# Row maxima of causal attention: the diagonal blocks masked on GpSimd after a copy by ScalarE, instead of by a matmul on TensorE

## The chip, the cores and the metric

The kernel runs as one program on one core of a Trainium2 chip. The metric is the device time of one execution in microseconds (us); the time of a kernel is the median of its runs. A profile is one further execution, recorded instruction by instruction. The engines are named as the profile names them: PE (TensorE, with PEld for its weight loads), DVE (VectorE), ACT (ScalarE), POOL (GpSimd) and SP (SyncE, which issues DMAs here).

## The reference

Two layers over 4096 tokens of width 256 (16 sequences of 256). Each layer adds to its input the output of a mixer and of a mixture of experts, both fed with the same layer norm. Layer 0 has a cumulative mixer with a gated unit and 32 experts of which a token takes four; layer 1 has causal attention with 16 heads of width 16 and eight experts of which a token takes two, and a shared one. The change lies in layer 1's attention, cut here to what matters:

```python
Q = (Xn @ Wq_w.T + Wq_b).reshape(b, s, H, D_K).transpose(0, 2, 1, 3)   # H = 16, D_K = 16, s = 256
K = V = Q
Qr = Q * cos + _rotate_half(Q) * sin
Kr = K * cos + _rotate_half(K) * sin
A = jnp.einsum('bhqd,bhkd->bhqk', Qr, Kr) / math.sqrt(D_K)
A = jnp.where(causal, A, -jnp.inf)
A = jax.nn.softmax(A, axis=-1)
O = jnp.einsum('bhqk,bhkd->bhqd', A, V)
```

The softmax needs, for each head and each query, the maximum of the scores over the keys that are not later than the query. Of a head's 256 x 256 scores in blocks of 128, the block of early queries and late keys is never needed, the block of late queries and early keys is needed whole, and the two blocks on the diagonal (a head's "own halves") are needed below the diagonal.

## The kernel before, in words

Tokens are worked in eight groups `g` of 512, each of two sequences `b`. All work is written as generators that yield steps: an engine, a cost in us, and options. `Weave` is a planner that runs when the kernel is built. It keeps a clock for each engine and takes, again and again, the step that can begin first, the smaller key at ties (`rush` lowers a step's key for such ties). Within a generator a step begins when the one before it has landed, which is its cost and a hop of 0.15 us later, unless that one is `aside`. `need` and `gives` are events, `get` and `put` are pools of buffers. The planned order is the order in which instructions stand on each engine, and engines work in order; semaphores hold an instruction until its inputs are there. Where a ready step asks for two or more of a pool, steps with a larger key may not take from that pool from the time it is ready (`first` and `behind`).

The pools that matter: `s`, the eight PSUM banks, and `mid`, 14 buffers of SBUF with 2 KB for each of 128 partitions. The experts' tiles take both: in layer 1 each of three lanes runs `expert_tile1` (transposes at L1207, `xhi` and `xlo` at L1212 and L1215, matmuls at L1229, `st` at L1240 to L1244, `thi` and `tlo` at L1247 and L1250, matmuls at L1256, `ry` at L1266, scatters of `y` on POOL at L1277), with `xr` gathered by POOL at L1185, three tiles ahead. Layer 0's dense part (`gated`, matmuls at L942 and L919, `sg` at L964 to L968) and the gathers of `yk` (L1054), the scatters of `perm` (L571, each behind a memset of one column at L570) and `combine` run beside the first groups' attention.

Attention of one `g, b` is `project`, then for each of four columns `c` (four heads) `maxima`, then `shifts`, which adds the maxima to the queries, and for each `c` `weigh`, which forms the scores anew with keys on the partitions (L1457), their exponentials (ACT, L1468), sets those above the diagonal to zero by a selection on POOL (L1474), multiplies by the values (L1486) and copies the result out (ACT, L1502; in the last group's second sequence DVE, L1497 and L1499). `shares` then divides by the sums by way of DMAs.

`maxima` takes four banks. Eight matmuls (L1408), one for each head and half of the queries, write a head's scores into the 384 columns of its bank: columns 0 to 127 are the early queries' own half, 128 to 255 the late queries against the early keys, 256 to 383 the late queries' own half. `masked` then adds for each head, by one bf16 matmul of `ident_b` with `mask_b` (L1397), 0 or -1e30 to the two own halves. DVE reduces each bank's three blocks to three maxima (L1419), which go to `tops`, and the bank is free. In `shifts` the late queries' two maxima are put together (L1437).

The generators' keys set the mix: `maxima` of `g, b, c` has 39 + 10 g + 4.5 b + 0.8 c, the experts' lanes of layer 1 begin at 70 and rise.

Of the kernel before, what the change touches and what calls it, by code (L numbers as in the profile page):

```python
# [13 lines left out]
ALU = mybir.AluOpType  # L14
AX = mybir.AxisListType
PSUM = bass.MemoryType.PSUM

P = 128
# [27 lines left out]
NEG = -1e30  # L46
# [161 lines left out]
def step(eng, cost, **o):  # L208
    return eng, cost, o
# [3 lines left out]
def two_layers(  # L213
# [6 lines left out]
    nc = tc.nc  # L220
# [27 lines left out]
    def mid(shape, name, dtype=F32):  # L248
        return work.tile(shape, dtype, tag="mid", name=name, bufs=MID)
# [3 lines left out]
    def bank(shape, i=0):  # L253

        n = shape[1] if len(shape) == 2 else shape[1] * shape[2]
        ap = banks[w.ids["s"][i]][: shape[0], :n]
        return ap if len(shape) == 2 else ap.rearrange("p (a b) -> p a b", a=shape[1])
# [16 lines left out]
    ident_b = const.tile([P, P], BF16, name="ident_b")  # L274
    mask_b = const.tile([P, 2 * P], BF16, name="mask_b")
# [17 lines left out]
    tops = [const.tile([P, H, 3], F32, name=f"tops{i}") for i in range(2)]  # L293
# [71 lines left out]
    RUSH = 40.0  # L365
# [929 lines left out]
    def rows_of(r):  # L1295
        return slice(HW * r, HW * (r + 1))
# [93 lines left out]
                nc.tensor.transpose(tp[:, i, j * P : (j + 1) * P], flat[:, j, c : c + P], ident)  # L1390
        return tp

    def masked(four, lhsT, rhs):

        for s in four:
            ends = s.rearrange("p (i n) -> p i n", n=P)[:, 0::2, :]
            nc.tensor.matmul(ends, lhsT=lhsT, rhs=rhs, start=False, stop=True)  # L1397

    def maxima(g, b, c):

        need = [("kT", g, b, c // 2), ("qT", g, b, c // 2)]
        yield step("PE", 1.4, get=["s"] * 4, need=need)
        kT, qT = qks[g, b]
        four = [bank([P, 3 * P], r) for r in range(4)]
        for i in range(2):
            n = (i + 1) * P
            for r in range(4):
                nc.tensor.matmul(  # L1408
                    four[r][:, i * P : i * P + n],
                    lhsT=qT[rows_of(r), c, i * P : (i + 1) * P],  # L1410
                    rhs=kT[rows_of(r), c, :n],
                    start=(i == 0),
                    stop=False,
                )
        masked(four, ident_b, mask_b)
        for r in range(4):
            yield step("DVE", 0.48, put=["s"], gives=[("max", g, b, c)] if r == 3 else [])

            nc.vector.tensor_reduce(  # L1419
                tops[b][:, c * 4 + r, :],  # L1420
                four[r].rearrange("p (i n) -> p i n", n=P),
                AX.X,
                ALU.max,
            )

    def shifts(g, b):


        for two in range(HC // 2):
            yield step("DVE", 0.43, need=[("max", g, b, 2 * two + i) for i in range(2)])  # L1430
            hs = slice(8 * two, 8 * two + 8)
            to = lambda j: peaks[:, j, :].rearrange("p (r w) -> p w r", w=HW)[
                :, 2 * two : 2 * two + 2, :
            ]
            of = lambda i: tops[b][:, hs, i].rearrange("p (c r) -> p c r", r=4)
            nc.vector.tensor_copy(to(0), of(0))
            nc.vector.tensor_tensor(to(1), of(1), of(2), ALU.max)  # L1437
            yield step("PE", 0.35, get=["s"])
            tp = bank([P, S])
            for j in range(2):  # L1440
                nc.tensor.transpose(tp[:, j * P : (j + 1) * P], peaks[:, j, :], ident)
            yield step("DVE", 0.61, put=["s"], gives=[("mT", g, b, two)])
            qT = qks[g, b][1][:, 2 * two : 2 * two + 2, :]
            nc.vector.tensor_tensor(  # L1444
                qT, qT, tp.unsqueeze(1).to_broadcast([P, 2, S]), ALU.add
            )
# [284 lines left out]
    for g in range(NG):  # L1731
# [3 lines left out]
        for b in range(GT // S):  # L1735
            at = DENSE[g] + 5 * b
# [32 lines left out]
    for g in range(NG):  # L1769
        early = max(DENSE[g] + 9, 34) + 0.5 * g  # L1770
        w.add(chosen(g), early)
        w.add(combine(g), early, 0.1)
        w.add(route1(g), early + 2, 0.1)
        w.add(spread(L1, g), early + 4)
        at = 38 + 10 * g
        w.add(room(g), at - 6)
        for b in range(GT // S):
            ab = at + 4.5 * b
            w.add(project(g, b), ab)
            for c in range(HC):  # L1780
                w.add(maxima(g, b, c), ab + 1 + c * 0.8)
                w.add(weigh(g, b, c), ab + 5 + c * 0.8)
            w.add(shifts(g, b), ab + 4.5)
            w.add(shares(g, b), ab + 8)
        w.add(half(g), at + 9)
        ready = [("aT", g, 0), ("po", g, 1, HC - 2)] if g == LAST[0] else [("aT", g, 1)]
        w.add(opened(NG + g, "o1", 2, ready), at + 12)
        for c in range(NC1):
            w.add(chunk(g, c), at + 12 + c)
        w.add(unpacked(g), at + 10)  # L1790
        w.add(attended(g), at + 14)
        w.add(closed1(g), at + 15)
        if g < LATE:
            w.add(finish(g), 130)
# [81 lines left out]
```

## Time and profile before

| | |
|---|---|
| median of 6 runs | 1654.29 us (1648.11 to 1661.16) |
| the profiled execution | 1666.46 us |
| its span, first to last instruction | 1664.0 us |
| mean granted TensorE clock | 0.910 |
| instructions in the span | 27711 |
| matmuls on PE | 9372 |
| mask matmuls (L1397) | 256 |
| reductions of maxima (L1419) | 256, from 788.6 to 1606.4 us |
| selections in `weigh` (L1474) | 64, from 823.4 to 1628.8 us; 1087 ns at least, median 1094, 1972 at most |
| layer 1's experts (L1207) | from about 1248 us on |

The page gives for each engine its busy time and share of the span. A group of instructions shows the line, engine and operation, the tile written and the tiles read, the shape and the number, then busy us and mean ns of one, and behind the second bar how long the engine had been idle just before them and what ended that. A window's row shows the busy time of each engine in that stretch and the granted clock, as a share of the full one. Matmuls overlap in PE's pipeline, so that the mean duration of one is longer than the distance from one to the next.

### The profile page before, as it was taken

Reading aid. Unit: us, or ns where it says so; the run is one execution under the profiler, and the core shown is the slowest. Engines: PE = TensorE matmul, PEld = TensorE weight load, DVE = VectorE, ACT = ScalarE, POOL = GpSimd, SP = SyncE. Lnnn points to the kernel's source line nnn. Section 1 sums busy time; section 2 is a strip of 40 time slices with the busy share of each in tenths; the row PEclk is TensorE's granted clock in tenths of the full one; section 3 lists DMA queues with packets and bytes.
Section 4 is the critical chain, followed back from the end, with each engine's and each line's share of the span. In section 5 each row is a group of like instructions: output and inputs, shape, how many; then the busy total and the mean of one; then the engine's idle time right before and its main releaser. Section 6 shows DMA issues by size and latency. Waiting matters only on the chain. (4 is left out here: it accounts for less than half of the span.)

```text
span 1664.0 us, 27711 instructions
## 1 busy us (share of the span) xinstructions
PE 1407.9 (85%) x9372; PEld 1117.9 (67%) x9372; DVE 972.6 (58%) x2505; ACT 693.3 (42%) x1521; POOL 829.3 (50%) x1086
## 2 busy tenths in 40 slices
PE   5889969889999997787799699786878888899975
PEld 3678857568898886666567587553546777777753
DVE  4988937574342432148847373675755575565757
ACT  4333312444564553223324132442344756664641
POOL 3477854564554552436663614354145556555530
PEclk8999989989999998888889799886879999898997
DMA  9211100258888888415532502243244344343368
GB/s 328 77 52 39 39 26 14 59 185 260 277 278 265 265 248 192 153 59 161 93 80 90 143 26 90 65 111 59 89 96 137 105 140 138 122 129 117 97 203 266
DMA packets 164069, 223.45 MB, mean 134 GB/s; under 512 B 29672, under 2 KB 120152, under 8 KB 163672
## 3 DMA queue, kind: packets, MB, share of 16 engines
q1 hardware_dynamic: 136152, 162.11, 31.8%
q0 software_dynamic: 27776, 59.58, 13.6%
q8 instruction: 74, 1.21, 0.3%
q14 instruction: 67, 0.55, 0.1%
HBM read 151.13 MB, written 66.22 MB: 131 GB/s over the span
## 5 line engine op out<-in xcount | busy, mean ns | idle before, releaser
L942 PE MATMUL bank<-yT,wsw 128*128 128x256 f32 x1024 | 244.3, 385 | 4.6 <-issue 3.5
L571 POOL DMA_INDIRECT perm<-pairs,at_u x192 | 192.3, 1002 | 95.5 <-DVE pairs L514 40.6
L744 POOL DMA_INDIRECT xr_ring<-rows_d,who x160 | 155.7, 973 | 158.3 <-PE bank L762 113.5
L942 PEld LDWEIGHTS bank<-yT,wsw 128*128 128x128 f32 x1024 | 194.6, 194 | 34.2 <-issue 7.1
L1474 POOL TENSOR_SCALAR_AFFINE_SELECT pT<-pT 128x1024 f32<-128x1024 f32 x64 | 72.9, 1141 | 218.9 <-ACT pT L1468 182.0
L919 PE MATMUL bank<-wdn,sg 128*128 128x256 f32 x512 | 136.9, 416 | 50.0 <-DVE sg L968 46.5
L1419 DVE TENSOR_REDUCE tops<-bank 128x3 f32<-128x384 f32 x256 | 131.2, 548 | 58.5 <-PE bank L1397 36.6
L1054 POOL DMA_INDIRECT yk<-y,slots x128 | 132.6, 1036 | 61.8 <-issue 35.6
L919 PEld LDWEIGHTS bank<-wdn,sg 128*128 128x128 f32 x512 | 103.4, 208 | 73.6 <-DVE sg L968 53.4
L1468 ACT ACTIVATE pT<-bank 128x384 f32<-128x384 f32 x256 | 110.8, 499 | 95.2 <-PE bank L1457 61.5
L767 DVE COPY xTr<-bank 128x512 f32<-128x512 f32 x80 | 54.4, 689 | 138.9 <-PE bank L762 97.9
L1277 POOL DMA_INDIRECT y<-ry,to x78 | 80.9, 1038 | 93.6 <-ACT ry L1266 81.0
L1408 PE MATMUL bank<-kT,qT 32*128 32x128 f32 (+1 forms) x1024 | 97.2, 400 | 32.9 <-ACT aT L1502 12.3
L964 ACT ACTIVATE sg<-bank 128x512 f32<-128x512 f32 x64 | 38.0, 596 | 146.2 <-PE bank L942 84.2
L1408 PEld LDWEIGHTS bank<-kT,qT 32*128 32x128 f32 x1024 | 58.4, 210 | 58.3 <-issue 19.4
L351 PE MATMUL bank<-wqkvsu,xnT 128*128 128x512 f32 (+1 forms) x256 | 97.4, 514 | 0.0
L1457 PE MATMUL bank<-qT,kT 32*128 32x256 f32 (+1 forms) x1024 | 76.6, 380 | 23.9 <-DVE qT L1444 12.0
L1185 POOL DMA_INDIRECT xr<-rows_d,who x78 | 79.0, 1013 | 31.5 <-issue 20.4
L1229 PE MATMUL bank<-xhi,w_ring 128*88 128x256 f32 x312 | 87.0, 308 | 5.7 <-issue 3.1
L798 ACT ACTIVATE ry<-bank,share 128x256 f32<-128x256 f32 x160 | 66.8, 470 | 50.7 <-PE bank L788 19.7
L1457 PEld LDWEIGHTS bank<-qT,kT 32*128 32x128 f32 x1024 | 56.8, 203 | 45.5 <-DVE qT L1444 12.6
L1229 PE MATMUL bank<-xlo,w_ring 128*88 128x256 f32 x312 | 83.0, 297 | 2.7 <-DVE xlo L1215 1.9
(270 smaller groups left out, 3241.6 us busy)
## 6 DMA issues: line engine op xcount, KB each, us to landing
w_ring<-in_wud SPq DMA_DIRECT2D x80, 256.0 KB
vones<-in_wud SPq DMA_DIRECT2D x80, 256.0 KB
y<-ry SPq DMA_DIRECT2D x80, 256.0 KB
w_b<-in_we SPq DMA_DIRECT2D x39, 304.0 KB
rows_d<-xn SPq DMA_DIRECT2D x16, 512.0 KB
xnT<-xnT_d SPq DMA_DIRECT2D x16, 512.0 KB
y1k<-y SPq DMA_DIRECT2D x16, 512.0 KB
x<-in_x SPq DMA_DIRECT2D x8, 512.0 KB
```

Source lines behind the costliest of these rows:

```text
L351: nc.tensor.matmul(ps_ap, lhsT=lhs(k), rhs=rhs(k), start=(k == 0), stop=(k == KC - 1))
L571: ins = nc.gpsimd.indirect_dma_start(out=la.perm, out_offset=bass.IndirectOffsetOnAxis(ap=la.at_u[:, c : c + 1], axis=0), in_=la.pairs[:, ...
L744: nc.gpsimd.indirect_dma_start(out=xr_ring[:, m % 3, i * D : (i + 1) * D], out_offset=None, in_=rows_d, in_offset=bass.IndirectOffsetOnAxi ...
L919: nc.tensor.matmul(oTs[o][j][:, t % 2, :], lhsT=lhs[:, t * P : (t + 1) * P] if lhs.shape[1] > P else lhs, rhs=rhs, start=(done == 0 and t ...
L942: nc.tensor.matmul(ap[:, i, :], lhsT=w_of[0](i, k), rhs=rhs[:, k, :], start=(i == 0 and k == 0), stop=(i == 1 and k == KC - 1),)
L1054: nc.gpsimd.indirect_dma_start(out=ys[g, k][:, t, :], out_offset=None, in_=y0, in_offset=bass.IndirectOffsetOnAxis(ap=L0.slots[:, c : c + ...
L1229: nc.tensor.matmul(h[:, c, :], lhsT=w_c(i // 2), rhs=(hi, lo)[i % 2][:, i // 2, :], start=(i == 0), stop=(i == n - 1),)
L1277: ins = nc.gpsimd.indirect_dma_start(out=y1, out_offset=bass.IndirectOffsetOnAxis(ap=L1.to[:, i, m : m + 1], axis=0), in_=y[:, i, :], in_o ...
L1408: nc.tensor.matmul(four[r][:, i * P : i * P + n], lhsT=qT[rows_of(r), c, i * P : (i + 1) * P], rhs=kT[rows_of(r), c, :n], start=(i == 0), ...
L1419: nc.vector.tensor_reduce(tops[b][:, c * 4 + r, :], four[r].rearrange("p (i n) -> p i n", n=P), AX.X, ALU.max,)
L1457: nc.tensor.matmul(four[r][:, q : q + n], lhsT=kT[rows_of(r), c, i * P : (i + 1) * P], rhs=mT[rows_of(r), c, i * P :], start=(i == 0), sto ...
L1468: nc.scalar.activation(pT[:, :, r, :], four[r].rearrange("p (b n) -> p b n", n=P), AF.Exp)
```

## The change

The mask matmuls go. The score matmuls of a call end with the late queries' ones. Then, for each of the four heads, ACT copies the two own halves out of the bank into a `mid` buffer that two heads share (`own`), and DVE reduces the middle block alone, straight from the bank, into the second of the head's three maxima; then the bank is free. For each pair of heads POOL selects in place, in the 512 elements of `own`, what is not above the diagonal and fills the rest with -1e30, and one reduction on DVE takes the first and third maximum of both heads at once. A call asks for two `mid` buffers with its four banks, and its planned costs are 0.95 us on PE (1.4 before), four times 0.37 on ACT, four times 0.22 and twice 0.65 on DVE (four times 0.48 before) and twice 0.62 on POOL, with `rush`.

```diff
-    def masked(four, lhsT, rhs):
-
-        for s in four:
-            ends = s.rearrange("p (i n) -> p i n", n=P)[:, 0::2, :]
-            nc.tensor.matmul(ends, lhsT=lhsT, rhs=rhs, start=False, stop=True)
-
     def maxima(g, b, c):
 
         need = [("kT", g, b, c // 2), ("qT", g, b, c // 2)]
-        yield step("PE", 1.4, get=["s"] * 4, need=need)
+        yield step("PE", 0.95, get=["mid", "mid"] + ["s"] * 4, need=need)
...
-                    stop=False,
+                    stop=(i == 1),
                 )
-        masked(four, ident_b, mask_b)
+
+        owns = [mid([P, 2, 2, P], "own") for _ in range(2)]
         for r in range(4):
-            yield step("DVE", 0.48, put=["s"], gives=[("max", g, b, c)] if r == 3 else [])
-
-            nc.vector.tensor_reduce(
-                tops[b][:, c * 4 + r, :],
-                four[r].rearrange("p (i n) -> p i n", n=P),
-                AX.X,
-                ALU.max,
-            )
+            of = four[r].rearrange("p (i n) -> p i n", n=P)
+            own = owns[r // 2]
+            yield step("ACT", 0.37, gives=[("own", g, b, c, r // 2)] if r % 2 else [])
+            nc.scalar.copy(own[:, r % 2, :, :], of[:, 0::2, :])
+
+            yield step("DVE", 0.22, put=["s"])
+            nc.vector.tensor_reduce(tops[b][:, c * 4 + r, 1:2], of[:, 1:2, :], AX.X, ALU.max)
+        for two, own in enumerate(owns):
+            yield step("POOL", 0.62, need=[("own", g, b, c, two)], rush=RUSH)
+            flat = own.rearrange("p r i k -> p (r i) k")
+            nc.gpsimd.affine_select(
+                out=flat, in_=flat, pattern=[[0, 4], [-1, P]],
+                compare_op=ALU.is_ge, fill=NEG, base=0, channel_multiplier=1,
+            )
+            yield step("DVE", 0.65, put=["mid"], gives=[("max", g, b, c)] if two else [])
+            at = c * 4 + 2 * two
+            nc.vector.tensor_reduce(tops[b][:, at : at + 2, 0:3:2], own, AX.X, ALU.max)
```

`ident_b` and `mask_b` are still loaded at the start.

## The prediction

> **What bounds the kernel now.** I read the page's first part, then the stages by window, the groups by line and form, the waits of PE, and the timeline of two calls of `maxima`. The page says which engine is nearest to full:
>
> ```profile
> PE 1407.9 (85%) x9372; PEld 1117.9 (67%) x9372; DVE 972.6 (58%) x2505; ACT 693.3 (42%) x1521; POOL 829.3 (50%) x1086
> ```
>
> A share over the whole span mixes stages, and the first maxima come at 787 us, the last at 1606. The windows table cuts the rest there (start and end, length, busy us of PE, PEld, DVE, ACT, POOL with instruction counts, granted clock, DMA share, GB/s):
>
> ```profile
> 787.00:900.00 113.00, 99.24 (x701) 73.42 (x700) 74.43 (x224) 40.35 (x83) 70.90 (x89) 0.88 0.46 98
> 900.00:1050.00 150.00, 125.52 (x762) 98.03 (x760) 69.72 (x201) 37.69 (x70) 58.69 (x72) 0.92 0.28 80
> 1050.00:1250.00 200.00, 156.07 (x1378) 106.40 (x1378) 140.11 (x403) 83.37 (x174) 78.11 (x95) 0.81 0.33 84
> 1250.00:1610.00 360.00, 320.46 (x2889) 258.52 (x2889) 223.72 (x405) 215.99 (x425) 193.93 (x257) 0.92 0.40 125
> 1610.00:1664.00 54.00, 25.17 (x216) 17.85 (x216) 33.53 (x35) 7.08 (x15) 4.85 (x4) 0.75 0.88 284
> ```
>
> PE is busy 0.88, 0.84, 0.78 and 0.89 of the first four stages, 64 calls lie in them (8, 8, 20 and 28), and no other engine passes 0.70. So PE is the bound, loosely where the granted clock is 0.81 and tightly from 1250 us. The groups by line and form price the instructions that matter (busy us, mean ns of one | idle before, releaser):
>
> ```profile
> L1419 DVE TENSOR_REDUCE tops<-bank 128x3 f32<-128x384 f32 x256 | 131.2, 548 | 58.5 <-PE bank L1397 36.6 <-remote 11.7 <-issue 9.5
> L1474 POOL TENSOR_SCALAR_AFFINE_SELECT pT<-pT 128x1024 f32<-128x1024 f32 x64 | 72.9, 1141 | 218.9 <-ACT pT L1468 182.0 <-issue 29.9 <-PE bank L1397 6.4
> L1397 PE MATMUL bank<-mask_b,ident_b 128*128 128x256 bf16 x256 | 45.8, 310 | 0.0
> L1486 PEld LDWEIGHTS bank<-pT,vones 128*32 128x32 f32 x1024 | 29.0, 116 | 46.3 <-issue 17.6 <-POOL pT L1474 10.7 <-POOL apart L570 7.5
> L1502 ACT COPY aT<-bank 128x256 f32<-128x256 f32 x60 | 22.4, 373 | 96.2 <-PE bank L1486 54.9 <-remote 19.8 <-PE bank L1229 9.5
> L550 DVE TENSOR_REDUCE pl<-oa 128x16 f32<-128x512 f32 x8 | 5.4, 680 | 0.1
> ```
>
> The timeline shows what a call's four mask matmuls hold (start us, us, engine, idle before in brackets):
>
> ```profile
> 1356.85 0.94 PE L1408 MATMUL bank<-kT,qT 32*128 32x128 f32 x16
> 1357.72 0.33 PEld L1397 LDWEIGHTS <-ident_b 128*128 128x128 bf16 x4 [0.33 <-issue]
> 1357.72 0.61 PE L1397 MATMUL bank<-mask_b,ident_b 128*128 128x256 bf16 x4
> 1358.09 0.36 PE L1229 MATMUL bank<-xhi,w_ring 128*88 128x256 f32 x1
> ```
>
> The next work starts at 1358.09, 0.37 us after the first mask matmul, although the four are drawn 0.61 long. The 0.33 ahead of them is the change from 32-row pieces to the full array; whatever full-array work comes next pays it too, so it stays.
>
> **PE's saving.** 256 mask matmuls go. By busy time they are 45.8 us. From the first mask matmul of each call to the start of the next matmul, read in the timeline for all 64 calls, the slots are 5.6, 4.7, 13.0 and 14.4 us in the four stages, 37.6 together; from first to fourth alone, 26.0. A slot saved is worth time only where PE would have been busy: by the shares above 5.6 x 0.88 + 4.7 x 0.84 + 13.0 x 0.78 + 14.4 x 0.89 = 31.8 us. That is the credit; 26.0 by the same shares gives 22.
>
> **What is added.** ACT: four copies a call of a head's two own halves, 128x256 out of a bank, at L1502's 373 ns: 256 x 0.373 = 95.5 us. POOL: two selections a call over 512 elements; L1474's median is 1094 ns for 1024, so between half of that with no fixed part (0.55) and 0.60 with the 0.11 us that a one-element memset on POOL takes (L570); I take 0.60: 128 x 0.60 = 77 us. DVE: instead of four reductions at 548 ns (2.19 us), four over 128 elements and two over 512. L1161's reductions of 64 elements take a median of 0.21, which is the floor; the straight line from there to L1419's 384 gives 0.28 for 128. L550 has 0.68 for 512. At 0.28 a call is 2.48 us, 0.29 more, 19 us in all; at 0.21 it is the same as before. I take 19.
>
> None of this work is on PE, and each engine has room (between 787 and 1610 us DVE is 62% busy, ACT 46%, POOL 49%). It is not free, because PE waits for these engines. From the waits of PE between 787 and 1610 us, it waits 53 us for DVE, 32 for ACT and 9.5 for POOL (the rows summed by engine), while they work 508, 377 and 402: 0.10, 0.084 and 0.024 us for each busy us. At those rates the added work costs 19 x 0.10 + 95.5 x 0.084 + 77 x 0.024 = 11.8 us, say 12. If the cover is poorer, with twice the rates, it is 24; if the earlier release of the banks outweighs it, nothing.
>
> **The new wait.** A masked maximum on DVE needs POOL's selection, and that needs two ACT copies. Behind a held maximum on DVE stand `xlo`, `st`, `tlo` and `sg` of the experts and the dense part, whose banks and operands PE waits for. POOL's selections wait in order as well; behind one stand the gathers of `xr` and `yk` and the scatters of `y`. With `xr` fetched three tiles ahead I cost that at nothing; without that cover it is up to 0.60 us for each. For DVE's hold the trace has no row. From below it is nothing (the selection was done long ago), from above 1.0 us or more, a selection behind one of POOL's DMA instructions of about 1.0 us. The nearest row is L1486, where weights wait for the same kind of selection: 10.7 us over 64, 0.17 each. That makes 128 x 0.17 = 21 us of hold on DVE. Between the 0.10 above (2 us) and all of it (21), I let 9 us reach PE, since DVE sits in every chain that frees banks.
>
> **Order and buffers.** `maxima` yields ACT, DVE, ACT, DVE and so on, each after the one before it has landed, so the planner's own call is longer: by its costs and its hop of 0.15, four reductions took 2.5 us behind PE and now the copies and reductions take 3.6, the selections with their maxima 3.1 more. Maxima run well ahead of `weigh`, which hides that, except for the last four calls at 1597 to 1606 us, where about 1.5 us come on top of the tail. Two `mid` buffers are held in a call; counted from first write to last read in the timeline, six to eight of the 14 are in use from 1250 us on, so I cost them at nothing. But the planner reserves what is asked for twice, and a `maxima` that waits for banks now also keeps `mid` from steps of later keys. With every cost changed, the whole order behind 787 us is dealt anew. What such a deal is worth the waits of PE show: single waits of 11.1 us (L1408 for `aT`), 9.4 (L1457 for `over`, behind an addition that waits for its DMA) and 9.3 (L919 for `sg`). I take nothing for it and allow 12 us to both sides.
>
> **The clock.** The stage with most calls for its work, 1050 to 1250 us, already has 0.81. If it fell to the 0.75 of the last row, its 156 us of PE would become 12 longer; if it rose to 0.88, 12 shorter. I take no change. [...]
>
> **Ports.** L1474's selections take 1087 ns at least and 1141 on average, so company on DVE costs 0.05 each, 6 us over 128 on POOL, which are covered. [...]
>
> **The sum.** 31.8 - 12 - 9 - 1.5 = 9.3 us off. The profiled execution is 1666.46 us (span 1664.0, 2.5 around it), 12.2 above the median of the six runs, 1654.29; the difference is taken over as it is, since the stages are the same: 1657.2 for that execution, 1645 for the median.
>
> **The rivals.** No change: the slots were only 26.0 and fall partly into waits, credit 22, against the same 22.5: 1655. For it speaks the loose stage at 0.81; against it 0.89 from 1250 us.
>
> Slower: DVE held by the masked maxima. POOL is busy 0.49 of the time between 787 and 1610, mostly in instructions of 1.0 us, so a selection comes 0.25 us late on average on top of the 0.17: 0.42 x 128 = 54 us of hold, of which three quarters reach PE, 40. Without the hold the change gains 18.3, so 1654.3 - 18.3 + 40 = 1676. It decides from 0.21 us for each of the 128 masked maxima that reach PE (18.3 + 8.3 = 26.6 us): then the time is up by over 0.5%. For it speak POOL's 182 us of waiting for ACT at L1474; against it the earlier release of banks.
>
> More than forecast: the added work is all covered and the hold is nil, 31.8 - 4: 1626. ACT's 0.44 speaks for it, the waits for `aT` against it.
>
> **Chances.** Forecast 0.34, more than forecast 0.10, no change 0.24, slower 0.32. About 0.5% (8.3 us) is what a measurement of this kernel can tell from no change. The range goes from the larger gain to the slower case with the 12 us of the order, less what is left out at both ends: 1624 to 1684; the likeliest case alone is 1633 to 1646.
>
> **What would show it.** Right: no L1397; PE some 46 us less busy with 9116 matmuls; 256 copies on ACT near 0.37, 128 selections on POOL near 0.60, DVE up by 10 to 20 us; PE's share between 1250 and the last maxima still above 0.85. The slower case: long idle times of DVE ahead of the masked maxima with POOL as releaser, and PE waiting for `sg`, `xlo`, `tlo` or banks. Wrong altogether: a stage whose clock has moved by over 0.05, or a tail behind the last maxima that is 10 us longer.

## The result, and the profile after

The kernel after takes 1677.53 us (median of 20 runs, 1662.18 to 1693.36), the kernel before beside it 1653.49 (46 runs, 1638.78 to 1665.1): a ratio of 1.0153 [1.0133, 1.0173] (in brackets, here and below, the 95% interval). The change makes the kernel about 24 to 25 us slower, where 9.3 us off were forecast. The time lies inside the range, and near the 1676 of the slower rival, but the experiments below show that it did not come about in that rival's way.

The profiled execution of after took 1674.32 us (span 1672.6), 3 below its median; that of before took 1666.46, above its median. So these two traces show only 8 of the 24 us. Their shapes can be compared; the sizes are taken from the timed runs.

The first part of the page after:

```profile
PE 1426.5 (85%) x9116; PEld 1129.3 (68%) x9116; DVE 995.6 (60%) x2633; ACT 768.5 (46%) x1777; POOL 916.1 (55%) x1214
```

256 matmuls are gone, and yet PE is busy 18.6 us longer, not 46 less. ACT has 75 us more, POOL 87, DVE 23. The windows table of after, with the cuts used for before (start and end, length, busy us and count of PE, PEld, DVE, ACT, POOL, granted clock, DMA share, GB/s); the last row ends 10 us later than before's:

```profile
787.00:900.00 113.00, 96.84 (x617) 70.62 (x609) 67.88 (x189) 45.58 (x106) 75.64 (x94) 0.73 0.36 79
900.00:1050.00 150.00, 131.28 (x791) 105.51 (x784) 87.40 (x267) 53.02 (x112) 66.96 (x86) 0.92 0.35 100
1050.00:1250.00 200.00, 158.02 (x1288) 110.78 (x1286) 135.61 (x399) 102.08 (x243) 105.99 (x137) 0.77 0.32 87
1250.00:1610.00 360.00, 312.58 (x2606) 247.60 (x2606) 217.72 (x433) 237.00 (x509) 218.02 (x301) 0.89 0.40 124
1610.00:1674.00 64.00, 42.66 (x348) 28.62 (x347) 46.32 (x64) 16.57 (x41) 17.04 (x12) 0.63 0.69 221
```

The clock column is the thing to see. Where before had 0.88, 0.92, 0.81, 0.92 and 0.75, after has 0.73, 0.92, 0.77, 0.89 and 0.63. The same matmul took longer at the lower clock (the 64 of 32x256 of `weigh` in the first stage, L1457 before and L1461 after: 461 ns on average at 0.88, 587 at 0.73), and that is where PE's busy time comes from. From the first maxima to the end, in one row for each kernel, before ahead of after:

```profile
787.00:1700.00 913.00, 726.46 (x5944) 554.23 (x5942) 541.50 (x1266) 384.48 (x766) 406.49 (x516) 0.88 0.38 110
```

```profile
777.00:1700.00 923.00, 748.03 (x5686) 567.79 (x5685) 564.20 (x1393) 458.42 (x1020) 492.59 (x642) 0.83 0.37 108
```

These windows end behind the kernel, and the time behind its end counts in them as full clock. Up to the end of its span PE idles for 150.5 us before and 147.6 after. Its busy time, each stretch weighted with the clock granted in it, is 649 us of work at the full clock before and 624 after. So PE has less work, idles as long, and is busy for 21.6 us more, because more of its work fell into times of a lower clock.

The groups that took the place of the mask matmuls (busy us, mean ns of one | idle before, releaser):

```profile
L1422 POOL TENSOR_SCALAR_AFFINE_SELECT own<-own 128x512 f32<-128x512 f32 x128 | 90.3, 712 | 41.7 <-ACT own L1415 40.4
L1415 ACT COPY own<-bank 128x256 f32<-128x256 f32 x256 | 88.5, 379 | 43.1 <-PE bank L1402 26.9
L1418 DVE TENSOR_REDUCE tops<-bank 128x1 f32<-128x128 f32 x256 | 70.8, 282 | 57.6 <-ACT own L1415 44.1
L1428 DVE TENSOR_REDUCE tops<-own 128x4 f32<-128x512 f32 x128 | 85.9, 677 | 12.7 <-POOL own L1422 8.9
```

The durations are those foreseen, but for the selections (712 ns on average, where 600 were taken). The last line is the rival's own place, and it is nearly empty: DVE idled 12.7 us ahead of the masked maxima, 8.9 of it for POOL. DVE idled longer ahead of the small reductions, 44.1 us for ACT's copies. Before, the group in that place (L1419) waited 36.6 us for PE.

The first transposes of layer 1's experts (L1207) run from 1240 to 1574 us (before from 1248 to 1585) and end 11 us earlier; what lies behind them takes 99 us instead of 79. The last four token groups start their scores 114 us apart on average (before, 105), and the last maximum starts at 1636.5 us instead of 1606.4, with the last scores of `weigh` at 1644 instead of 1627. Up to the experts' start nothing was lost: 787 to 1248 before, 777 to 1240 after.

PE's waits in the same stretch as in the prediction, 787 to 1610 us, add up to 76.5 us for DVE (before 53), 22.7 for ACT (32) and 5.7 for POOL (9.5). The longest entries (us in total, times, longest us):

```profile
PE bank L919 <- DVE sg L968: 15.3, 3, 7.6
PE bank L1461 <- DVE qT L1448: 9.3, 5, 4.0
PE bank L1402 <- ACT qT L1381: 7.4, 1, 7.4
PE bank L1445 <- DVE peaks L1441: 6.7, 4, 5.0
```

PE waits in them for `sg`, `qT` and the peaks, a few long waits each. None of its waits in this stretch names the masked maxima (L1428); those for the middle blocks' maxima (L1418) sum to 6.1 us, against 5.9 for the maxima before (L1419).

### The profile page after: what moved, and what is told of

Read it like the earlier page. It is cut to its first block, busy times and chain, and to the rows that moved or that the text cites. A ratio compares the mean times of both kernels' runs of the same rounds, so it can differ in the third digit from the quotient of the medians.

```text
span 1672.6 us, 27994 instructions
## 1 busy us (share of the span) xinstructions
PE 1426.5 (85%) x9116; PEld 1129.3 (68%) x9116; DVE 995.6 (60%) x2633; ACT 768.5 (46%) x1777; POOL 916.1 (55%) x1214
## 5 line engine op out<-in xcount | busy, mean ns | idle before, releaser
L1402 PE MATMUL bank<-kT,qT 32*128 32x256 f32 (+1 forms) x1024 | 102.3, 419 | 27.6 <-ACT qT L1381 7.4
L1461 PE MATMUL bank<-qT,kT 32*128 32x256 f32 (+1 forms) x1024 | 102.3, 431 | 23.9 <-DVE qT L1448 11.8
L1422 POOL TENSOR_SCALAR_AFFINE_SELECT own<-own 128x512 f32<-128x512 f32 x128 | 90.3, 712 | 41.7 <-ACT own L1415 40.4
L1461 PEld LDWEIGHTS bank<-qT,kT 32*128 32x128 f32 x1024 | 74.0, 236 | 57.2 <-issue 18.0
L1415 ACT COPY own<-bank 128x256 f32<-128x256 f32 x256 | 88.5, 379 | 43.1 <-PE bank L1402 26.9
L1418 DVE TENSOR_REDUCE tops<-bank 128x1 f32<-128x128 f32 x256 | 70.8, 282 | 57.6 <-ACT own L1415 44.1
L1402 PEld LDWEIGHTS bank<-kT,qT 32*128 32x128 f32 x1024 | 63.1, 223 | 51.3 <-issue 17.4
L1428 DVE TENSOR_REDUCE tops<-own 128x4 f32<-128x512 f32 x128 | 85.9, 677 | 12.7 <-POOL own L1422 8.9
```

Of the source, the lines that this page charges most:

```text
L1402: nc.tensor.matmul(four[r][:, i * P : i * P + n], lhsT=qT[rows_of(r), c, i * P : (i + 1) * P], rhs=kT[rows_of(r), c, :n], start=(i == 0), ...
L1415: nc.scalar.copy(own[:, r % 2, :, :], of[:, 0::2, :])
L1422: nc.gpsimd.affine_select(out=flat, in_=flat, pattern=[[0, 4], [-1, P]], compare_op=ALU.is_ge, fill=NEG, base=0, channel_multiplier=1,)
L1428: nc.vector.tensor_reduce(tops[b][:, at : at + 2, 0:3:2], own, AX.X, ALU.max)
L1461: nc.tensor.matmul(four[r][:, q : q + n], lhsT=kT[rows_of(r), c, i * P : (i + 1) * P], rhs=mT[rows_of(r), c, i * P :], start=(i == 0), sto ...
```

## Experiments

The theories were: (M) the credit for the masks is small or absent, since PE is paced by its clock and by others' chains; (A) the work added on ACT, POOL or DVE costs more than its share; (O) the re-dealt order costs; (H) DVE is held by masked maxima behind POOL, the rival. Every ratio is to runs of the kernel before on the same chip. The runs are spread over five chips: on two of them the kernel before takes 1490 us (mean clock 0.948), on three 1652 to 1674 (0.911 to 0.916), so ratios are compared, not times, and a comparison of two chips is weaker than one on the same chip. Where a run is said to have the order of before or of the changed kernel, its trace has it: DVE, ACT and POOL take the instructions that both kernels have in the same order, and PE does but for a few score matmuls that change places with a neighbour.

### The masks alone

**nomask_old_order** and **nomask_again** (the same kernel on two chips): the kernel before without its mask matmuls, in before's order.

```diff
-                    stop=False,
+                    stop=(i == 1),
-        masked(four, ident_b, mask_b)
```

> The kernel before without its 256 mask matmuls and with nothing in their place, so that the maxima are taken over the unmasked diagonal blocks; the planned costs and the order are those of before. It tells what PE's saving alone is worth. By the prediction's credit it is 22 to 32 us faster than before, 1622 to 1632. [...] If the credit stands, the whole loss must come from what was added or from the order.

> The kernel before without its mask matmuls once more, with more rounds, on the same chip as the three others: it is the base for the run with the copies from a constant. 0.9935 as before, between 0.989 and 0.998. Its granted clock lies about 0.010 below that of before, as in the first run; the prediction's credit, 0.981 to 0.987, is excluded if the interval stays above 0.988.

Measured: 0.9935 [0.9891, 0.998] on the first chip, 11 us; 0.9996 [0.9973, 1.0019] on the second, nothing. The mean granted clock fell with it both times: 0.8994 against 0.9106, and 0.9365 against 0.948. The row from the first maxima to the end on the first chip:

```profile
793.00:1700.00 907.00, 704.66 (x5686) 542.71 (x5685) 539.07 (x1265) 383.93 (x764) 405.89 (x514) 0.87 0.39 110
```

The masks took 21.8 us of busy time with them (726.5 to 704.7). Weighted with the clock as above it is 649 to 621, so 28 us of work at the full clock, near the 26.0 that lay between first and fourth mask matmul. About 11 of these became time on the first chip and none on the second; both intervals exclude the 22 of the low credit. So M holds: most of the credit was never there.

**nomask_new_cost**: the same, with the plan told the shorter PE step.

```diff
-        yield step("PE", 1.4, get=["s"] * 4, need=need)
+        yield step("PE", 1.00, get=["s"] * 4, need=need)
```

> The same without masks, but the planner is told 1.0 us for the score matmuls of a call where it was told 1.4, so that the order behind the first maxima is dealt anew; no operation is added. It tells what a new deal is worth with the same work. By the prediction's allowance it lies within 12 us of the one with the old order. If a new deal alone can cost the 24 us that were lost, it can lie as far above.

Measured: 1.002 [0.9978, 1.0063]. One planned cost, and with it another deal of the order, takes back the 0.65% that leaving out the masks gave (the medians of the two runs, on the same chip, lie 13 us apart).

**after_filled** is the other direction: the changed kernel, with eight matmuls of 128 columns a call into an unused part of the banks, as many columns as the four masks had.

```diff
+        for i in range(8):
+            spare = banks[w.ids["s"][i % 4]][:, 3 * P :]
+            nc.tensor.matmul(spare, lhsT=ident_b, rhs=mask_b[:, :P], start=False, stop=(i >= 4))
```

> The changed kernel, and behind the scores of each call eight bf16 matmuls of 128x128 by 128 columns into the unused last quarter of the four banks, where the mask matmuls stood: as many columns for PE as the masks, with no use. Same plan. If PE's work were what counts (the prediction's credit), it is 22 to 32 us slower than the changed kernel. [...]

**after_again** and **after_third** are the changed kernel as it is, the first in this set.

> The changed kernel as it is, so that its ratio to before is known on the chip that the next three runs have. Both theories expect 1.013 to 1.022.

> The changed kernel as it is, on the chip of the run beside it. 1.015 to 1.022 of before.

Measured: after_filled 1.0154 [1.0082, 1.0225], after_again 1.0174 [1.0096, 1.0251], after_third 1.0165 [1.0118, 1.0213]. Useless columns put back on PE cost nothing that four runs of each can tell: the medians of after_again and after_filled, on the same chip, are 1678.2 and 1678.6 us, which excludes the 22 to 32 us of the credit but not a cost of some 10. The mean clock rose by 0.014 (0.9053 against 0.891). after_filled, then after_again, from the first maxima on:

```profile
770.00:1700.00 930.00, 773.55 (x6225) 596.41 (x6225) 569.46 (x1411) 462.70 (x1026) 499.72 (x651) 0.86 0.39 110
```

```profile
770.00:1700.00 930.00, 740.45 (x5712) 564.45 (x5711) 568.61 (x1407) 461.47 (x1026) 497.23 (x650) 0.85 0.39 109
```

PE is busy for 33 us more. These two profiled executions are 16.8 us apart (1685.86 and 1669.05), though the medians agree, so the traces put 16 of the 33 us into gaps that PE had anyway; by the timed runs it is all of them, within some 10 us.

### The order alone

**old_ops_new_order**: the steps, costs and buffers of the changed kernel, with the mask matmuls and one reduction over three blocks as before. ACT's, POOL's and the last DVE steps are planned and hold nothing.

```diff
             yield step("ACT", 0.37, gives=[("own", g, b, c, r // 2)] if r % 2 else [])
-            nc.scalar.copy(own[:, r % 2, :, :], of[:, 0::2, :])
             yield step("DVE", 0.22, put=["s"])
-            nc.vector.tensor_reduce(tops[b][:, c * 4 + r, 1:2], of[:, 1:2, :], AX.X, ALU.max)
+            nc.vector.tensor_reduce(tops[b][:, c * 4 + r, :], of, AX.X, ALU.max)
...
             yield step("POOL", 0.62, need=[("own", g, b, c, two)], rush=RUSH)
-            nc.gpsimd.affine_select(
...
```

> The changed kernel's steps, costs, buffers and so its planned order, but the operations of before: the mask matmuls behind the scores, one reduction of three blocks where the middle block's stands; the copies, selections and pair maxima are steps with nothing in them. Theory one (the order): the loss is in the order, with attention's last groups behind the experts; then it is as slow as the changed kernel or slower by the mask matmuls, 1675 to 1700. Theory two (the operations): the loss is DVE, ACT and POOL holding each other; then it is near before, 1645 to 1665.

Measured: 1.0173 [1.0086, 1.0259], with not one new instruction. Its row from the first maxima on has as many instructions as before's, and PE busy for 760.2 us instead of 726.5, for nearly the same work at the full clock (656 us, before 649) and as much idle time (151.7 and 150.5):

```profile
786.00:1700.00 914.00, 760.19 (x5942) 575.32 (x5941) 538.75 (x1265) 385.73 (x764) 404.18 (x514) 0.86 0.38 109
```

Its planned costs (0.95 and 0.22) are not those of its operations, though, which could be the reason by itself. Two more runs set that apart.

**old_ops_newer_order**: the same without the two `mid` buffers that a call reserves.

```diff
-        yield step("PE", 0.95, get=["mid", "mid"] + ["s"] * 4, need=need)
+        yield step("PE", 0.95, get=["s"] * 4, need=need)
```

> The changed kernel's steps and planned costs with the operations of before, as in the run old_ops_new_order (1.0173), but the two mid buffers of a call are not asked for, so that nothing is kept from steps with later keys beyond the banks. If the reservation made the order bad, it is at 1.005 or below; if the planned row of ACT, DVE, POOL and DVE steps did, it stays at 1.012 or more.

**old_ops_row**: the kernel before with its own operations and costs, and only the longer row in the plan: an empty ACT step ahead of each reduction, two empty POOL steps and the later `max` behind them.

```diff
-            yield step("DVE", 0.48, put=["s"], gives=[("max", g, b, c)] if r == 3 else [])
+            yield step("ACT", 0.37)
+            yield step("DVE", 0.48, put=["s"])
...
+        for two in range(2):
+            yield step("POOL", 0.62, rush=RUSH)
+            yield step("DVE", 0.0, lat=0.8, gives=[("max", g, b, c)] if two else [])
```

> The operations of before with their right planned costs (1.4 us on PE, 0.48 for each reduction), and with the change's extra steps planned between and behind them, empty: 0.37 on ACT ahead of each reduction, twice 0.62 on POOL, and the maxima there 0.8 us behind each of these. The runs old_ops_new_order and old_ops_newer_order had costs in the plan that their operations did not have (0.95 on PE, 0.22 on DVE). If the longer row of steps makes a bad order, this one is at 1.008 or more of before; if those were slow since their plan was wrong on PE and DVE, it is at 1.003 or below.

Measured: old_ops_newer_order 1.013 [1.0095, 1.0164], old_ops_row 1.013 [1.0092, 1.0167]. Without the reservation of `mid` the planner deals the same order on DVE, ACT and POOL, so the reservation did not make it, and old_ops_new_order and old_ops_newer_order show one order to be slow on two chips. The order of old_ops_row is another one: with the right costs a longer row can be dealt as badly, 1.3% or 21 us. That does not show that the row made the changed kernel's order slow, since in nomask_new_cost one planned figure cost 0.8%.

**before_late_max**: the kernel before, whose plan has a call's maxima come 3.7 us later, and nothing else.

```diff
-            yield step("DVE", 0.48, put=["s"], gives=[("max", g, b, c)] if r == 3 else [])
+            yield step("DVE", 0.48, put=["s"])
...
+        yield step("idle", 0.0, lat=3.7, gives=[("max", g, b, c)])
```

> The kernel before with nothing changed but one figure in the plan: the event that the maxima of a call are there comes 3.7 us later, which is what the change's longer row of steps adds by the planner's costs. Same operations, same costs of each. Theory one, sharpened: the next group's attention of a sequence may only start when this group's has ended (the at0 and at1 buffers), so that a later maximum lengthens the period of the groups; then this is slower than before by over 0.5%, with 110 us or more from one group's scores to the next behind 1250 us, where before has 103 to 108. If latency is covered, as the prediction had it, it is within 0.5%.

Measured: 0.9938 [0.9908, 0.9968], faster. The later maxima are not what costs. What is left of the row is ACT's and POOL's time in the plan and the longer hold of the four banks there, or the chance of one deal; which of them it is was not told apart.

### The operations alone, in before's order

**new_ops_old_order**: before's plan, with all the new operations: the four copies stand right behind the scores, the reductions in before's four DVE steps, and selection and shared maximum behind each second one.

```diff
-                    stop=False,
+                    stop=(i == 1),
-        masked(four, ident_b, mask_b)
...
+        owns = [mid([P, 2, 2, P], "own") for _ in range(2)]
+        for r in range(4):
+            ends = four[r].rearrange("p (i n) -> p i n", n=P)[:, 0::2, :]
+            nc.scalar.copy(owns[r // 2][:, r % 2, :, :], ends)
         for r in range(4):
             yield step("DVE", 0.48, put=["s"], gives=[("max", g, b, c)] if r == 3 else [])
-            nc.vector.tensor_reduce(tops[b][:, c * 4 + r, :], ...)
+            nc.vector.tensor_reduce(tops[b][:, c * 4 + r, 1:2], of[:, 1:2, :], AX.X, ALU.max)
+            if r % 2:
...
+                nc.gpsimd.affine_select(out=flat, in_=flat, ...)
+                nc.vector.tensor_reduce(tops[b][:, at : at + 2, 0:3:2], own, AX.X, ALU.max)
...
```

> The opposite: the planner deals the order of before (costs and steps of before, two mid buffers taken aside), and the new operations stand where the old ones stood: four copies on ACT behind the scores, the middle block's reduction in each DVE step, and behind every second one POOL's selection and, right behind it on DVE, the maximum of the pair. Theory one (the order): faster than before, 1630 to 1650. Theory two (the operations): slow, 1670 to 1700, here with DVE waiting for POOL at once in each pair, so that the hold is the longest that the change can make.

Measured: 1.0106 [1.0014, 1.0197]. Against the 0.9935 of nomask_old_order in the same set the new operations cost 1.7%, 28 us, in an order that doesn't know of them. Its row:

```profile
791.00:1700.00 909.00, 735.40 (x5686) 558.49 (x5685) 561.08 (x1393) 460.39 (x1022) 488.47 (x642) 0.84 0.38 110
```

PE does the same 5686 matmuls as in nomask_old_order, on the same chip, and is busy 30.7 us longer at 0.84 instead of 0.87. Weighted with the clock as above, its work is 622 us in both, and up to the end of the span it idles for 166.8 us against 164.2. So nearly the whole loss is matmuls at a lower clock. The new operations put no work on PE and hardly lengthen its idle time in sum (by 2.6 us); how they lower the clock was not shown.

**nomask_copies** and **nomask_copies_selects**: the kernel without masks, with four unread copies a call on ACT, and with the two selections on POOL as well.

```diff
...
+        for r in range(4):
+            ends = four[r].rearrange("p (i n) -> p i n", n=P)[:, 0::2, :]
+            nc.scalar.copy(owns[r // 2][:, r % 2, :, :], ends)
```

> The kernel before in its own order without the mask matmuls, and with the four copies of each call on ACT alone added, whose result nobody reads; the maxima are still reduced from the bank over all three blocks, unmasked, by one reduction on DVE for each head. So only ACT has more work, 95 us, and a bank is free when both ACT and DVE have read it. The same without copies ran at 0.9935 of before, with copies, selections and the divided reductions at 1.0106. If the copies in the way of the banks are the price, this is at 1.003 or more; if POOL and DVE are, it stays below 0.998.

> The same with POOL's two selections for each call on the copies as well, which nobody reads either; DVE is as before. If POOL's 90 us in its queue, with the scatters and gathers behind them, are the price, it is 0.005 or more above the one with copies alone; if the divided reductions on DVE and their wait for POOL are, it is level with it and the step to 1.0106 is still missing.

Measured: 1.0227 [1.0142, 1.0312] with the copies, 1.012 [1.0088, 1.0152] with copies and selections. The selections add nothing; why the run with more work came out the faster one is open. On this chip there is no run without masks and copies: against nomask_old_order (0.9935) on another the copies cost 1.9 to 2.9%, against nomask_again (0.9996) 1.2 to 2.3%, with nobody reading what they write. The divided reductions add nothing to that in new_ops_old_order (1.0106). The copies can cost in two ways: by holding the score banks longer, or by standing in ACT's queue.

**nomask_act_busy** takes the banks away: the same copies read a constant.

```diff
-            ends = four[r].rearrange("p (i n) -> p i n", n=P)[:, 0::2, :]
-            nc.scalar.copy(owns[r // 2][:, r % 2, :, :], ends)
+            held = cst[:, : 2 * P].rearrange("p (i n) -> p i n", n=P)
+            nc.scalar.copy(owns[r // 2][:, r % 2, :, :], held)
```

> The kernel without masks, in the old order, with the four copies a call on ACT at the same places and of the same size, but from a constant in SBUF instead of from the banks: ACT has the same extra work, and no bank waits for it. Without copies the ratio to before was 0.9935, with copies from the banks 1.0227. If ACT's queue is the price (what stands behind the copies comes later), this is at 1.005 or more; if the later release of the banks is, it stays below 0.998.

Measured: 1.0144 [1.011, 1.0178], against 0.9996 for nomask_again in the same set: 1.5%, 22 us of 1490, on the same chip. These copies wait for no matmul and ACT never idled ahead of them; the group's line:

```profile
L1421 ACT COPY own<-cst 128x256 f32<-128x256 f32 x256 | 84.9, 418 | 0.0
```

The stage of layer 1's experts, 1102 to 1410 us in nomask_again and 1111 to 1436 in nomask_act_busy, has the same work in it but for ACT's copies (the windows rows, nomask_again first):

```profile
1102.00:1410.00 308.00, 283.38 (x2700) 229.63 (x2701) 223.24 (x409) 213.05 (x422) 199.29 (x257) 0.96 0.46 142
```

```profile
1111.00:1436.00 325.00, 290.50 (x2702) 232.28 (x2702) 223.79 (x409) 245.46 (x533) 198.81 (x257) 0.94 0.44 134
```

It takes 17 us longer for the same 2700 matmuls, with 32 us more on an ACT that is still idle for a quarter of the stage. Some of ACT's lateness is seen one engine on: DVE's `tlo` waits for ACT's `thi`, and its wait goes from 12.6 us to 19.0 (nomask_again first):

```profile
L1250 DVE TENSOR_TENSOR tlo<-st,thi 88x512 fp32r<-88x512 f32 x39 | 28.8, 741 | 13.6 <-ACT thi L1247 12.6 <-PE bank L1229 0.9
```

```profile
L1250 DVE TENSOR_TENSOR tlo<-st,thi 88x512 fp32r<-88x512 f32 x39 | 29.2, 750 | 21.4 <-ACT thi L1247 19.0 <-ACT own L1421 1.4 <-PE bank L1229 0.8
```

DVE's wait for ACT's part of `st` goes from 28.1 to 31.5 us. From there it does not reach PE as waiting: PE's waits for DVE are 57.7 and 57.4 us from the first maxima on, and those for ACT go from 14.6 to 22.3. The rest is in PE's busy time (nomask_again first; the windows again end behind the kernels):

```profile
715.00:1700.00 985.00, 672.24 (x5690) 521.11 (x5689) 541.85 (x1269) 383.10 (x766) 413.84 (x516) 0.93 0.35 102
```

```profile
715.00:1700.00 985.00, 686.32 (x5692) 528.15 (x5691) 542.43 (x1270) 460.21 (x1025) 413.11 (x518) 0.91 0.36 102
```

Up to the end of its span the second trace is 26 us longer: PE idles for 12 of them, and for 14 it is busy with the same work (614 and 617 us at the full clock) at a mean clock of 0.89 instead of 0.91. The copies also keep two `mid` buffers of each call, which this run does not take apart from ACT's time; the waits of all engines for these copies sum to 5.8 us.

### The rival: DVE held by POOL

**after_no_select**: the changed kernel without its selections, so that the masked maxima are taken over unmasked halves and wait for ACT alone.

```diff
-            nc.gpsimd.affine_select(
-                out=flat, in_=flat, pattern=[[0, 4], [-1, P]],
-                compare_op=ALU.is_ge, fill=NEG, base=0, channel_multiplier=1,
-            )
```

> The changed kernel in its own order, without POOL's 128 selections (the step stays in the plan, with nothing in it, and the maxima are those of the unmasked blocks). DVE's pair maxima then wait for ACT alone and POOL has 77 to 90 us less work. The prediction's slower case (DVE held behind POOL): it is faster than the changed kernel by 20 us or more, near before. Theory one (the order): less than 8 us faster.

**after_piped**: the changed kernel with ACT's four copies planned as a row of their own, beside DVE's reductions instead of between them. **after_piped_rush** gives these steps the urgency that POOL's have.

```diff
-            yield step("ACT", 0.37, gives=[("own", g, b, c, r // 2)] if r % 2 else [])
+            yield step("ACT", 0.37, aside=True, gives=[("copied", g, b, c, r)] + ...)
             nc.scalar.copy(own[:, r % 2, :, :], of[:, 0::2, :])
...
+        for r in range(4):
...
-            yield step("DVE", 0.22, put=["s"])
+            yield step("DVE", 0.22, aside=True, put=["s"], need=[("copied", g, b, c, r)])
```

> The changed kernel with the same operations, but its four copies are planned one behind the other on ACT, and the four reductions of middle blocks beside them, instead of copy, reduction, copy, reduction, each after the one before has landed. The planned call is shorter by some 2 us. Theory one: attention's period gets shorter and it is faster than the changed kernel by 5 to 15 us. Theory two (the operations hold each other): no difference above 5 us.

> The same, and the copies, reductions and pair maxima are taken ahead of other steps that could begin at the same time, as the selections already are. Theory one: a little faster again, up to 10 us below the one without. Theory two: no difference, or slower, as the experts' copies wait behind them.

Measured: after_no_select 1.0208 [1.0139, 1.0277], after_piped 1.0204 [1.0141, 1.0267], after_piped_rush 1.0216 [1.0157, 1.0275]. All three ran on one chip, on which the changed kernel itself was not run; elsewhere it has 1.0153 to 1.0174. With no selection there is nothing on POOL for DVE to be held by, and DVE did not idle ahead of these maxima:

```profile
L1424 DVE TENSOR_REDUCE tops<-own 128x4 f32<-128x512 f32 x128 | 85.2, 675 | 0.0
```

Yet the kernel is no faster than the changed one is on the other chips, and the trace of the changed kernel has only 8.9 us of such a hold. H falls as the cause of the loss. The two other orders of a call's copies and reductions are no faster either; each is a new deal of the whole order, so they don't tell what the order inside a call is worth by itself.

### A version that beats both

**nomask_late_max**: the kernel before without masks, with before_late_max's plan. Its maxima are taken over the unmasked own halves, so the shift of a row can be larger than its masked maximum. The softmax divides such a shift out again, as long as the exponentials of the allowed scores do not underflow.

```diff
-                    stop=False,
+                    stop=(i == 1),
-        masked(four, ident_b, mask_b)
...
+        yield step("idle", 0.0, lat=3.7, gives=[("max", g, b, c)])
```

> Two edits that each gave less time, together: no mask matmuls (0.9935), and the maxima planned 3.7 us later (0.9938), so that the planner deals another order with the same costs. If they add, 0.987 and the fastest kernel of this study; if the second one's gain was that of one deal for its own sum of work, it lies anywhere between 0.987 and 1.002.

Measured: 0.9917 [0.9889, 0.9945]. Most of it is the plan, as far as two chips can be compared: before_late_max alone has 0.9938 on the other one of 1490 us, and the masks on this chip are worth nothing (0.9996, nomask_again).

## Why the prediction was wrong

**What bounds the kernel.** "PE is the bound" was read from its busy share, 0.78 to 0.89 by stage, and the credit rests on that. PE's busy time contains the granted clock (from the first maxima on 726 us for 649 at the full clock before, 748 for 624 after), so a share of it is not a price of work. Of 28 us of matmuls at the full clock, leaving them out gave 11 us on one chip and none on another; putting as many columns in cost nothing that could be told, to within some 10 us.

**The credit (31.8 us, low 22).** Measured 11 and about 1 (0.04% of 1490). The working took each slot saved as time in proportion to PE's busy share. This step failed. The mean clock was lower by 0.011 in both runs: 28 us of work at the full clock took only 21.8 us of busy time away in nomask_old_order, and some 14 of these became idle time of PE.

**The clock ("I take no change").** This step failed. The changed kernel's mean clock is 0.889 over its timed runs, the kernel before's 0.911 to 0.916; the first stage of maxima fell from 0.88 to 0.73. The sign that was named as "wrong altogether", a stage whose clock has moved by over 0.05, is there. In the two pairs of traces that share a chip and an order, the same work of PE at a lower clock makes up 31 of 33 us (new_ops_old_order against nomask_old_order) and 14 of 26 (nomask_act_busy against nomask_again), so what was put at nothing was the larger part there. What lowered the clock stays open: after_filled has 0.014 of it back and no time.

**The added work (12 us, bounds 0 and 24).** Mis-sized, most of all for ACT: 95.5 us at 0.084 made 8.0 us; the copies' time on ACT, without banks, cost 22 us in nomask_act_busy, above the 16 that twice the rate gives. As a price of waiting the rate was good: PE's waits for ACT rose by 7.7 us there. It left out that PE's own matmuls took longer at a lower clock, 14 us in that pair (0.89 instead of 0.91). POOL's selections were rightly costed at little: the 1.0227 without them and 1.012 with them show no cost.

**The hold (9 us, and the rival's 40).** It had no row in the trace before, and the row that it has now is 12.7 us, 8.9 from POOL, below the 21 of the estimate. Leaving out the selections gained nothing that the runs show. That the measured time lies near the rival's 1676 is luck: other losses are of its size.

**The order (nothing, 12 to both sides).** This step failed. With the old operations the changed kernel's order costs 1.3 to 1.7%, 21 to 29 us, outside the 12 allowed. The longer row of `maxima` was seen, but only its last four calls were priced (1.5 us). A row is 6.7 us long in the plan at every one of the 64 calls, and its maxima ran less far ahead: the last of them starts 7.5 us before the last scores of `weigh`, where before it was 20. Whether that is what makes the order slow was not shown. The named sign of a longer tail behind the last maxima did not come, since the maxima themselves end 30 us later.

**The sum.** The costs do not add: the order alone is worth 1.013 to 1.017, the operations alone in the old order 1.0106, and both together 1.015 to 1.017. Why they do not add was not shown. With nothing to 11 us for the masks, and about 22 for ACT's copies or 21 for the order, the prediction would have ended slower.

**What was right.** L1397 is gone and 9116 matmuls are left; copies take 379 ns (373 foreseen), reductions 282 and 677 (280 and 680), so the straight line between two shapes was good. PE's share between 1250 and 1610 us is 0.87, above the 0.85 that was named, and says nothing of the loss. The change to the full array ahead of the next work stayed, as foreseen: in nomask_old_order no weight load of 88 or 128 rows came less than 0.33 us behind the last one of the scores, nor did one in the trace after, in the 53 calls where such a load stood next. DVE's busy time rose by 23 us, just above the 10 to 20 that were named. Selections take 712 ns on average and 646 at the median, against 600: more than half of the 1094 for twice the size, so the fixed part is larger than the 0.11 taken. Company on DVE shows as well: the 22 selections with no instruction of DVE beside them took 647 ns on average, the other 106 took 725; in the trace before the 10 of L1474 without took 1093, the other 54 took 1150.

## What to carry to other kernels

Price work on a busy TensorE by leaving it out in a kernel of its own, not by its busy time: here 28 us of matmuls were worth 11 us and none. Work on an engine with room (here ACT, 46% busy) is not priced by TensorE's waits for it alone: of 26 us lost, 8 were such waits and 14 were TensorE's own matmuls at a lower clock, so compare busy time and clock of the same matmuls as well. In a kernel whose order is dealt from planned costs, every edit of a step also deals again, here worth 0.6% better to 1.7% worse by itself; run the new order with the old work before any reason is sought in the instructions.

## What the hardware showed that was not expected

The granted clock did not rise when PE had less to do. It was lower with the mask matmuls gone (0.8994 against 0.9106 in nomask_old_order, 0.9365 against 0.948 in nomask_again), and higher with useless matmuls put in (0.9053 in after_filled, 0.891 in after_again). Nor did it follow PE's busy share from stage to stage: in the first four stages before, PE was busy for 0.88, 0.84, 0.78 and 0.89 of the time at a clock of 0.88, 0.92, 0.81 and 0.92; after, for 0.86, 0.88, 0.79 and 0.87 at 0.73, 0.92, 0.77 and 0.89. What sets the clock was not shown.

Chips differ by 11% on the same kernel: 1490 us at a mean clock of 0.948 on two, and 1652 to 1674 at 0.911 to 0.916 on three. The clock is the smaller part of it: ahead of the first maxima PE is busy for 681 us of 787 in the trace of before and for 664 of 717 in that of nomask_again, whose work up to there is the same; why PE idles less there was not looked into.
